# Copies, scalings and block differences go on whichever of two engines the list has free first

## The chip, the cores and the metric

The kernel runs on one core of a Trainium2 chip. A core has a matrix engine (TensorE, PE in the profile; its loading of weights is PEld), three engines for elementwise work (VectorE or DVE, ScalarE or ACT, GpSimd or POOL), a synchronising engine whose queue issues most DMAs (SyncE, SP), an on-chip memory (SBUF) and eight accumulator banks (PSUM). PE writes to the banks; DVE and ACT read them. In this kernel POOL works on SBUF alone. Each engine runs its own instructions in program order and waits on semaphores for the others.

The metric is device time in microseconds of one execution, the median of several runs.

## What is computed

The input x is 16 sequences of 256 tokens with 128 features, in float32. Six residual steps follow, each on a layer norm (no affine) of the running x:

```python
x = x + 0.5 * ffn(norm(x))          # L0: silu(x w1) * (x w2) -> gelu(h h1) -> gelu(h h2) -> w3; 128 -> 512 -> 512 -> 512 -> 128
x = x + nonlocal_attn(norm(x))      # (theta phi^T / sqrt(128)) g, no softmax
x = x + 0.5 * ffn(norm(x))          # the same weights again
x = x + 0.5 * experts(norm(x))      # two of 8 rank-64 experts, chosen by the first token of each sequence
x = x + attention(norm(x))          # 16 heads of 8, rotary positions, causal softmax
x = x + 0.5 * experts(norm(x))
```

Each weight of the feed-forward part is ternary with a scale per output; the attention has scores, a causal mask, softmax, a product with the values and an output projection.

## The kernel before

x stays in SBUF as 32 tiles of 128 tokens. The 16 sequences are worked in nine batches, seven of two sequences (n = 4 tiles, N = 512 tokens wide) and two of one (n = 2, N = 256).

**Feed-forward** (`ffn`, line 329). Features lie on the partitions, tokens along the row. Four chunks give silu(w1) x w2 into `h`. The two 512 x 512 layers are done by a Strassen scheme with seven block products instead of eight (lines 423 on). For it the list needs four differences of blocks of `h`, called T1 to T4 (`sums`, line 360): T1 on DVE, T2 to T4 on POOL; a copy of the first product out of PSUM (`left`, line 384, on ACT); five sums with PSUM (`sum_of`, on DVE, rows `h<-h,pb`); and four gelus on ACT. Each product is four matmuls in the program, eight records in the trace.

**Norms** (`normed`, line 265). DVE makes statistics (`st`, `mv`), POOL makes `nm`, `ve`, `rstd` and `shift` in four small instructions, ACT makes `xn`, one instruction per tile. PE transposes xn and DVE copies the result out of PSUM as `xnT` (`by_feature`, line 280).

**Attention** (`attention`, line 652). PE makes rotated inputs for keys and queries; DVE multiplies by cosine and sine and shuffles pairs, POOL adds (`rotary`, line 633, tile `rot`). From the keys ACT makes four masked planes (`keys`, line 678, rows `qkv<-rot,kone,kmask`), from the queries DVE makes two (`queries`, line 688, rows `qkv<-rot,qmask`). ACT copies the values out of PSUM (`vm`). For each block of scores PE fills four banks; DVE adds the causal mask in PSUM (`pb<-pb,causal`) and takes the row maxima (`mx<-pb`); PE makes the scores again with the maxima folded in, ACT takes the exp (`pr<-pb`), POOL masks (`pr<-pr`) and PE multiplies by the values.

**Non-local attention and experts.** `product` (line 504) makes three small matrices (`gram`, `gph`, `eff`), each copied out of PSUM by DVE. `gated` (line 532) chooses two experts: small DVE instructions, a tanh on ACT, gathers of the expert weights by POOL's own DMA queue (`ab`), and a weight `gw` on DVE.

**The list.** The order of the instructions on each engine is computed while the program is built. Each part above is a generator that yields steps: an engine, a price in us, the banks and buffers it takes and gives back, and what it needs and sets. `begin` (line 927) works out when each waiting step could start on the clock of its engine, and the loop at the end takes the earliest; among PE steps within 0.05 us the feed-forward chain comes last, so it fills what attention leaves. `issue` (line 975) emits the step and moves the engine's clock by the price; what depends on it is ready a `HOP` later (0.24, 0.15, 0.12 and 0.08 us for PE, ACT, DVE and POOL). A step of DVE on N columns is priced at 0.07 + 0.00105 N, of ACT at 0.16 + 0.00083 N, of POOL at 0.19 + 0.0021 N; `sums` prices its POOL steps at 0.05 + 0.002 N. A change of ACT's function table costs 1.28, and an exp that needs one is held back by 2.0 (`PATIENCE`). Nothing in the list tells of one elementwise engine slowing another. `find` (line 914) chooses the bank that is clear first; the first four, which the score blocks need all together, count as `LOAN` = 2.0 us later for anything else while feed-forward work is left. The feed-forward chain (`main`) doesn't use them at all then.

All instructions go out through one wrapper (line 220), which keeps them in the list's order, so nearly every row of the profile has the line L220; rows are told apart by their tiles.

Of the kernel before, what the change touches and what calls it, by code (L numbers as in the profile page):

```python
# [14 lines left out]
AF = mybir.ActivationFunctionType  # L15
# [4 lines left out]
P = 128  # L20
# [4 lines left out]
WARM = 10  # L25
GATHER = 1.15
LANDING = 2.2
LOAN = 2.0
PATIENCE = 2.0
SLACK = 0.05  # L30
HOP = {"PE": 0.24, "ACT": 0.15, "DVE": 0.12, "POOL": 0.08}
# [23 lines left out]
def macaron_kernel(ctx: ExitStack, tc: tile.TileContext, a: dict, out: bass.AP):  # L55
# [169 lines left out]

    def step(engine, us, table=None, banks=0, take=(), drop=(), after=None, needs=(), sets=(), tiles=None, lag=0.0):
        return dict(
            engine=engine, us=us, table=table, banks=banks, take=take, drop=drop, after=after, needs=needs, sets=sets, lag=lag,  # L230
            tiles=tiles,
        )

    def pe(us, **kw):
        return step("PE", us, **kw)
# [29 lines left out]
    def normed(t0, n, needs=()):  # L265
        yield step("DVE", 0.12 + 0.26 * n, needs=needs)
        st = sml.tile([P, GT, 6], F32, name="st")
        for t in range(n):
            nc.vector.bn_stats(st[:, t, :], x[:, t0 + t, :])
        mv = scales(st, n)  # L270
        yield step("POOL", 1.2 + 0.17 * n)
        rstd, shift = inverse(mv, n)
        (xn,) = yield step("ACT", 0.39 * n, take=("xn",))
        for t in range(n):
            nc.scalar.activation(
                xn.t[:, t, :], x[:, t0 + t, :], AF.Identity, bias=shift[:, t : t + 1], scale=rstd[:, t : t + 1]
            )
        return xn

    def by_feature(n, xn, keep=False):  # L280
        pt, xnT = yield pe(0.11 * n, banks=1, take=("xnT",), drop=() if keep else (xn,))
        v = pt.t.rearrange("p (t n) -> p t n", n=P)
        for t in range(n):
            nc.tensor.transpose(v[:, t, :], xn.t[:, t, :], ident)
        yield dve(n * P, drop=(pt,))
        nc.vector.tensor_copy(xnT.t[:, : n * P], pt.t[:, : n * P])
        return xnT

    def first_input(n):
# [39 lines left out]
    def ffn(which, t0, n):  # L329
# [29 lines left out]

        def sums(l, h, T):  # L360

            for i, e, x, y, needs in (
                (1, "DVE", (0, 1), (0, 0), ()),
                (2, "POOL", (1, 1), 1, ()),
                (3, "POOL", (1, 1), (0, 1), ()),
                (4, "POOL", (1, 0), 2, (("P6", l, me),)),
            ):
                needs += tuple(k for b in (x, y) if type(b) is tuple for k in has(l, *b))
                made = (("T", i, l, me),)
                drop = (T[2],) if i == 4 else ()  # L370
                (T[i],) = yield (
                    dve(N, needs=needs, take=("T",), sets=made, drop=drop) if e == "DVE"
                    else step("POOL", 0.05 + 0.002 * N, needs=needs, take=("T",), sets=made, drop=drop)
                )
                engine = nc.vector if e == "DVE" else nc.gpsimd
                engine.tensor_tensor(
                    T[i].t[:, :, :M], block(h, *x), T[y].t[:, :, :M] if type(y) is int else block(h, *y), ALU.subtract
                )

# [3 lines left out]

        def left(l, a, nh):

            yield act(N, sets=(("P1", l, me),))
            nc.scalar.copy(block(nh, 1, 1), in_two(a))

        def shared(l, b, d, nh):

# [108 lines left out]
    def nonlocal_attn(t0, n):  # L499
# [4 lines left out]
        def product(us, lhs, rhs, name, drop=()):  # L504

            (bk,) = yield pe(us, banks=1, drop=drop)
            pp = bk.t[:, : 2 * D].rearrange("p (b d) -> p b d", b=2)
            for b in range(nb):
                if lhs is None:
                    for t in range(2):  # L510
                        v = xn.t[:, 2 * b + t, :]
                        nc.tensor.matmul(pp[:, b, :], v, v, start=(t == 0), stop=(t == 1))
                else:
                    nc.tensor.matmul(pp[:, b, :], lhs[:, b, :], rhs, start=True, stop=True)
            yield dve(nb * D, drop=(bk,))
            m = sml.tile([P, 2, D], F32, name=name, bufs=1)
            nc.vector.tensor_copy(m[:, :nb], pp[:, :nb])
            return m

        gram = yield from product(0.45 * nb, None, None, "gram", (xn,))  # L520
# [72 lines left out]
    def experts(sg):  # L593
        xn = yield from normed(sg.t0, sg.n, (("ffn", 0, (1, sg.t0)), ("ffn", 1, (1, sg.t0)), ("constants",)))
        xnT = yield from by_feature(sg.n, xn)
        if sg.first:
            nb = len(sg.parts)
            yield step("POOL", 0.2 + 0.1 * nb)
            cls = sml.tile([P, 2, P], F32, name="cls", bufs=2)
            nc.gpsimd.tensor_copy(  # L600
                cls[:, :nb],
                xnT.t[:, : sg.n * P].rearrange("p (b s) -> p b s", b=nb)[:, :, 0:1].to_broadcast([P, nb, P]),
            )
            merged["before", sg.g] = yield from gated(nb, cls)
            yield step(None, 0.0, sets=(("before", sg.g),))
        yield from applied(("before", sg.g), sg, xnT)

    def gated_ahead(g, nb, y):
# [14 lines left out]
        pc = bk.t[:, : 2 * D].rearrange("p (b d) -> p b d", b=2)  # L623
        for b in range(nb):
            nc.tensor.matmul(pc[:, b, :], y[:, b, :], ones, start=True, stop=True)
        yield dve(nb * D, drop=(bk,))
        cls = sml.tile([P, 2, P], F32, name="cls", bufs=2)
        nc.vector.tensor_copy(cls[:, :nb], pc[:, :nb])
        merged["after", g] = yield from gated(nb, cls)
        yield step(None, 0.0, sets=(("after", g),))  # L630

# [1 line left out]
    def rotary(c0, N, xnT, n, rot):  # L633
# [10 lines left out]

        yield dve(N)
        nc.vector.stream_shuffle(rot[:, 1, :N], rot[:, 1, :N], [i ^ 1 for i in range(32)])
        yield pool(N)
        nc.gpsimd.tensor_tensor(rot[:, 0, :N], rot[:, 0, :N], rot[:, 1, :N], ALU.add)

    kept = {}  # L650

    def attention(sg):
# [25 lines left out]
        def keys():  # L678


            yield from rotary(c0, N, xnT, 1, rot.t[:, 0:2, :])
            for j in (0, 2, 1, 3):
                yield step("ACT", 0.28 + 0.00083 * N, sets=(("km", sg.t0, j),) + ((("kept", g),) if j == 3 and sg.first else ()))
                nc.scalar.activation(
                    km[:, PLANE[j], c0 : c0 + N], kT[:, :N], AF.Identity, bias=kone[:, j : j + 1], scale=kmask[:, j : j + 1]
                )

        def queries():

            yield from rotary(c0, N, xnT, 0, rot.t[:, 2:4, :])  # L690
            yield step(None, 0.0, sets=(("q", sg.t0),))
            for v in range(2):
                yield step("DVE", 0.15 + 0.0005 * N, sets=(("qz", sg.t0, v),))
                nc.vector.tensor_scalar(qz[:, v, c0 : c0 + N], qT[:, :N], qmask[:, v : v + 1], None, ALU.mult)
            yield step(None, 0.0, needs=(("km", sg.t0, 3),), drop=(rot,))

        spawn(keys())
# [3 lines left out]
        for t in range(n):  # L701
            nc.tensor.matmul(pv[:, t, :], xnT.t[:, t * P : (t + 1) * P], wvT, start=True, stop=True)
        v0 = sg.parts[0][1][0]
        yield step("ACT", 0.53 + 0.225 * n, drop=(bk,), sets=(("v", sg.t0),))
        for i in range(2):
            nc.scalar.copy(
                vm.t[:, v0 : v0 + n].rearrange("p t r (i h) c -> p (t r) i h c", i=2)[:, :, i, :, 16 * i : 16 * i + DK],
                pv[:, :n].rearrange("p t (r i h c) -> p (t r) i h c", i=2, h=2, c=DK)[:, :, i],
            )
# [204 lines left out]
    def find(n, short):  # L914
# [9 lines left out]
        best = min(some, key=lambda b: b.clear + (LOAN if not ended[0] and b in bank[:4] else 0.0))  # L924
        return best.clear, [best], None

    def begin(line):

        n = line.next
# [8 lines left out]
            t = max(t, find(n["banks"], line is not main)[0])  # L938
        if n["table"] == "exp" and table[0] != "exp" and not ended[0]:
            t += PATIENCE  # L940
        return max(t, clock[n["engine"]]) if n["engine"] else t


# [31 lines left out]
    def issue(line):  # L975
# [3 lines left out]
        since, banks, quad = find(n["banks"], line is not main)  # L979
        bufs = [min(store_of[r], key=lambda s: s.clear) for r in n["take"]]  # L980
        t = max([t, since] + [s.clear for s in bufs])
        e, us = n["engine"], n["us"]
        if e:
            if n["table"] and n["table"] != table[0]:
                table[0] = n["table"]
# [156 lines left out]
```

## Time and profile before

| | us |
|---|---|
| median of 3 runs (972.97 to 973.29) | 973.13 |
| the profiled execution: its time | 972.04 |
| its span, first instruction to last | 970.4 |
| PE busy | 918.1 |
| DVE busy | 646.1 |
| ACT busy, of it 77 table loads | 450.2, 98.8 |
| POOL busy | 371.8 |

A row of a group has: line, engine, operation, out<-in by tile name, size of one, x how many, then busy time and mean ns of one, then the engine's idle time ahead of them and what ended it. `pb` is any PSUM bank. The mean is the time from an instruction's start to its end; neighbours on DVE and ACT overlap by some 0.08 to 0.1 us, so their spacing is shorter. A line of waits has who waited, for whom, the total, how many times, and the longest. A line of a stretch has its limits, its length, then busy time of PE, PEld, DVE, ACT and POOL, the granted clock of PE, and the DMA share. A line of the timeline has start, length, engine and instruction. PE's granted clock was full but for the first slices (mean 0.996).

### The profile page before, as it was taken

How to read it: one execution, taken by the hardware profiler on the slowest of the kernel's cores; microseconds unless marked ns; L12 is line 12 of the kernel's file. 1: busy time of each engine (PE TensorE's matmuls, PEld its weight loads, DVE VectorE, ACT ScalarE, POOL GpSimd, SP SyncE). 2: the span in 40 equal slices, each digit the busy share in tenths (PEclk: the TensorE clock that was granted, in tenths of full speed). 3: DMA queues.
4: the chain of work that ended last, by engine and by line, in shares of the span. 5: the costliest groups of instructions: out<-in, count | busy, mean ns of one | idle time of the engine just before them, and what ended most of it. 6: DMA issues, size and time to landing. Idle time of an engine off the chain costs nothing.

```text
span 970.4 us, 16624 instructions
## 1 busy us (share of the span) xinstructions
PE 918.1 (95%) x6600; PEld 690.0 (71%) x6600; DVE 646.1 (67%) x1470; ACT 450.2 (46%) x672; POOL 371.8 (38%) x572
## 2 busy tenths in 40 slices
PE   6999999999999999999999999999999899898887
PEld 4877878666676767686786667767777777786565
DVE  5654456937687646857569376856577676869673
ACT  2244344365535463553552755254652547472342
POOL 5422334241534225341553425242444135343342
PEclk9999999999999999999999999999999999999999
DMA  7000000000000000000000000000000000000000
GB/s 249 16 1 1 1 12 7 5 1 2 12 23 1 1 1 22 12 1 1 13 22 1 2 12 1 23 1 1 12 12 11 1 12 2 23 7 12 1 22 7
DMA packets 14717, 13.76 MB, mean 14 GB/s; under 512 B 2032, under 2 KB 12080, under 8 KB 14640
## 3 DMA queue, kind: packets, MB, share of 16 engines
q1 hardware_dynamic: 12624, 8.11, 2.8%
q0 software_dynamic: 1600, 4.20, 1.5%
q8 instruction: 52, 0.85, 0.4%
q10 hardware_dynamic: 416, 0.39, 0.1%
q14 instruction: 25, 0.20, 0.1%
HBM read 10.60 MB, written 2.10 MB: 13 GB/s over the span
## 4 chain that ended last, share of the span: by engine, by line
PE 65%; DVE 18%; ACT 7%; issue 4%; POOL 3%; DMA 1%; SPq 1%; DVEq 0%; ACTq 0%; POOLq 0%
PE pb L220 65%; DVE mx L220 4%; DVE h L220 3%; ACT pr L220 3%; DVE pb L220 2%; ACT L220 2%; ACT xn L220 1%; POOL rstd L220 1%; DVE st L220 1%; DVE x L220 1%; DMA w3s<-in_w3T_dram 1%; DVE T L220 1%; ACT sil L220 1%; DVE den L220 1%; DVE gw L220 1%
## 5 line engine op out<-in xcount | busy, mean ns | idle before, releaser
L220 DVE TENSOR_TENSOR h<-h,pb 128x512 f32<-128x512 f32 (+1 forms) x180 | 111.9, 622 | 104.4 <-PE pb L220 98.7
L220 PE MATMUL pb<-T,hS 128*128 128x256 f32 (+1 forms) x576 | 134.5, 366 | 10.7 <-DVE h L220 5.8
L220 ACT ACTIVATE h<-h 128x512 f32<-128x512 f32 (+1 forms) x108 | 62.4, 581 | 173.7 <-DVE h L220 173.6
L220 POOL TENSOR_TENSOR T<-h,T 128x512 f32<-128x512 f32 (+1 forms) x72 | 83.7, 1163 | 122.5 <-DVE T L220 56.8
L220 PE MATMUL pb<-qkv 32*128 32x256 f32 (+2 forms) x1536 | 115.1, 405 | 14.9 <-ACT pr L220 7.6
L220 POOL TENSOR_SCALAR nm<-mv 128x4 f32<-128x4 f32 (+3 forms) x62 | 15.1, 243 | 274.1 <-DVE mv L220 267.4
L220 PEld LDWEIGHTS pb<-T,hS 128*128 128x128 f32 x576 | 95.0, 190 | 33.4 <-issue 8.1
L220 ACT ACTIVATE pr<-pb 128x1536 f32<-128x1536 f32 x64 | 92.4, 1449 | 54.6 <-PE pb L220 47.2
L220 ACT ACT_TABLE_LOAD x77 | 98.8, 1283 | 39.2 <-PE pb L220 36.3
L220 POOL TENSOR_SCALAR_AFFINE_SELECT pr<-pr 128x512 f32<-128x512 f32 x128 | 78.2, 635 | 100.0 <-ACT pr L220 99.7
L220 ACT ACTIVATE xn<-x,shift,rstd 128x128 f32<-128x128 f32 x188 | 77.7, 483 | 79.3 <-POOL shift L220 73.6
L220 DVE TENSOR_REDUCE mx<-pb 128x8 f32<-128x2048 f32 (+1 forms) x64 | 111.8, 1750 | 0.5
L220 DVE TENSOR_TENSOR pb<-pb,causal 128x1024 f32<-128x1024 f32 x64 | 78.5, 1227 | 36.1 <-PE pb L220 33.6
L220 PEld LDWEIGHTS pb<-qkv 32*128 32x128 f32 x1536 | 68.2, 184 | 48.1 <-ACT pr L220 16.0
L220 PE MATMUL pb<-xnT,w1T 128*128 128x512 f32 (+1 forms) x144 | 69.0, 561 | 3.0 <-ACT sil L220 1.5
L220 PE MATMUL pb<-xnT,w2T 128*128 128x512 f32 (+1 forms) x144 | 68.7, 559 | 1.3 <-ACT sil L220 1.0
L220 DVE SCALAR_TENSOR_TENSOR h<-pb,s,sil 128x512 f32<-128x512 f32 (+1 forms) x72 | 48.2, 684 | 31.1 <-ACT sil L220 21.2
L220 PE MATMUL pb<-T,h2T 128*128 128x256 f32 (+1 forms) x288 | 64.8, 362 | 3.3 <-DVE T L220 3.0
L220 PE MATMUL pb<-T,h1T 128*128 128x256 f32 (+1 forms) x288 | 66.3, 360 | 0.6 <-DVE T L220 0.6
L220 DVE TENSOR_TENSOR x<-x,pb 128x256 f32<-128x256 f32 (+2 forms) x79 | 37.4, 474 | 43.0 <-PE pb L220 42.8
L220 PE MATMUL pb<-h,h1T 128*128 128x256 f32 (+1 forms) x288 | 65.3, 364 | 0.2 <-DVE h L220 0.2
L220 PE MATMUL pb<-h,hS 128*128 128x256 f32 (+1 forms) x288 | 65.4, 360 | 0.0
(121 smaller groups left out, 1558.3 us busy)
## 6 DMA issues: line engine op xcount, KB each, us to landing
out_dram<-x SPq DMA_DIRECT2D x7, 256.0 KB, 2.3
x<-in_x_dram SPq DMA_DIRECT2D x6, 256.0 KB, 4.7
h1T<-in_h1T_dram SPq DMA_DIRECT2D x1, 1024.0 KB, 9.3
h2T<-in_h2T_dram SPq DMA_DIRECT2D x1, 1024.0 KB, 10.1
ab<-in_eab_dram,at POOLq DMA_INDIRECT x32, 2.8
x<-in_x_dram SPq DMA_DIRECT2D x3, 128.0 KB, 4.9
w1T<-in_w1T_dram SPq DMA_DIRECT2D x1, 256.0 KB, 3.9
w2T<-in_w2T_dram ACTq DMA_DIRECT2D x1, 256.0 KB, 4.1
```

Source lines behind the costliest of these rows:

```text
L220: return lambda *args, **kw: tc.keep_in_program_order(getattr(self.engine, name)(*args, **kw))
```

## The change

A step may now have two forms, each with an engine and a price (`either`). `pick` chooses the form that would end first: the later of the step's readiness and the engine's clock, plus price, plus that engine's hop. It is asked when the list looks for the next step and again when the step is issued. `SPARED`, which would count DVE as later, is 0.

Two forms are given to: xn (ACT 0.39 per tile or DVE 0.21); xnT, gram, gph, eff and one cls, the copies out of PSUM (DVE or ACT); the first product's copy `left` (ACT or DVE); all four differences T (DVE or POOL, POOL now priced 0.19 + 0.0021 N); the other cls (POOL or DVE); the rotary sum (POOL or DVE); the key planes (ACT or DVE); the query scalings (DVE or ACT); and the value copies (ACT 0.53 + 0.225 n or DVE 0.2 + 0.135 n). `LOAN` goes from 2.0 to 1.0. What is computed stays the same.

```diff
-LOAN = 2.0
+LOAN = 1.0
+SPARED = 0.0
...
+    chosen = [None]
+    def either(*alt, **kw):
+        return step(alt[0][0], alt[0][1], alt=alt, **kw)
+    def by():
+        return {"ACT": nc.scalar, "DVE": nc.vector, "POOL": nc.gpsimd}[chosen[0]]
+    def copied(n, **kw):
+        return either(("DVE", 0.07 + 0.00105 * n), ("ACT", 0.16 + 0.00083 * n), **kw)
+    def copy(to, src):
+        if chosen[0] == "ACT":
+            nc.scalar.copy(to, src)
+        else:
+            nc.vector.tensor_copy(to, src)
+    def scaled_by(to, src, scale, bias=None):
+        if chosen[0] == "ACT":
+            nc.scalar.activation(to, src, AF.Identity, scale=scale, **({} if bias is None else {"bias": bias}))
+        elif bias is None:
+            nc.vector.tensor_scalar(to, src, scale, None, ALU.mult)
+        else:
+            nc.vector.tensor_scalar(to, src, scale, bias, ALU.mult, ALU.add)
...
-        (xn,) = yield step("ACT", 0.39 * n, take=("xn",))
+        (xn,) = yield either(("ACT", 0.39 * n), ("DVE", 0.21 * n), take=("xn",))
...
-        yield dve(n * P, drop=(pt,))
-        nc.vector.tensor_copy(xnT.t[:, : n * P], pt.t[:, : n * P])
+        yield copied(n * P, drop=(pt,))
+        copy(xnT.t[:, : n * P], pt.t[:, : n * P])
...
-                (T[i],) = yield (
-                    dve(N, needs=needs, take=("T",), sets=made, drop=drop) if e == "DVE"
-                    else step("POOL", 0.05 + 0.002 * N, needs=needs, take=("T",), sets=made, drop=drop)
+                (T[i],) = yield either(
+                    ("DVE", 0.07 + 0.00105 * N), ("POOL", 0.19 + 0.0021 * N), needs=needs, take=("T",), sets=made, drop=drop
                 )
...
-            yield act(N, sets=(("P1", l, me),))
-            nc.scalar.copy(block(nh, 1, 1), in_two(a))
+            yield copied(N, sets=(("P1", l, me),))
+            copy(block(nh, 1, 1), in_two(a))
...
-        yield pool(N)
-        nc.gpsimd.tensor_tensor(rot[:, 0, :N], rot[:, 0, :N], rot[:, 1, :N], ALU.add)
+        yield either(("POOL", 0.19 + 0.0021 * N), ("DVE", 0.07 + 0.00105 * N))
+        by().tensor_tensor(rot[:, 0, :N], rot[:, 0, :N], rot[:, 1, :N], ALU.add)
...
-                yield step("ACT", 0.28 + 0.00083 * N, sets=(("km", sg.t0, j),) + ((("kept", g),) if j == 3 and sg.first else ()))
+                yield either(("ACT", 0.28 + 0.00083 * N), ("DVE", 0.15 + 0.0005 * N), sets=(("km", sg.t0, j),) + ((("kept", g),) if j == 3 and sg.first else ()))
...
-                yield step("DVE", 0.15 + 0.0005 * N, sets=(("qz", sg.t0, v),))
+                yield either(("DVE", 0.15 + 0.0005 * N), ("ACT", 0.28 + 0.00083 * N), sets=(("qz", sg.t0, v),))
...
-        yield step("ACT", 0.53 + 0.225 * n, drop=(bk,), sets=(("v", sg.t0),))
+        yield either(("ACT", 0.53 + 0.225 * n), ("DVE", 0.2 + 0.135 * n), drop=(bk,), sets=(("v", sg.t0),))
...
+    def pick(n, t):
+        if n["alt"]:
+            n["engine"], n["us"] = min(n["alt"], key=lambda a: max(t, clock[a[0]]) + a[1] + HOP[a[0]] + (SPARED if a[0] == "DVE" else 0.0))
```

## The prediction

> **What bounds the kernel now.** I read the page's busy line first, then busy time by stretch, then what TensorE (PE) waited for in each stretch, then single places in the timeline. The busy line and the chain of the page:
>
> ```profile
> PE 918.1 (95%) x6600; PEld 690.0 (71%) x6600; DVE 646.1 (67%) x1470; ACT 450.2 (46%) x672; POOL 371.8 (38%) x572
> ...
> PE 65%; DVE 18%; ACT 7%; issue 4%; POOL 3%; DMA 1%; SPq 1%; DVEq 0%; ACTq 0%; POOLq 0%
> ```
>
> PE is busy 918.1 of 970.4 us, and the change gives it no work and takes none away. So all there is to win is PE's idle time, 52.3 us. What there is to lose is open. Busy time by stretch (columns PE, weight loads, DVE, ACT, POOL) places it:
>
> ```profile
> 0.00:20.00 20.00, 12.08 (x39) 7.91 (x40) 8.75 (x32) 4.95 (x10) 9.98 (x21) 0.93 0.73 241
> 20.00:750.00 730.00, 712.07 (x4672) 528.97 (x4674) 484.03 (x1084) 345.25 (x516) 283.83 (x410) 1.00 0.03 9
> 750.00:850.00 100.00, 92.16 (x810) 74.10 (x806) 73.00 (x172) 53.00 (x84) 35.83 (x63) 0.98 0.03 9
> 850.00:970.40 120.40, 101.80 (x1084) 79.00 (x1084) 80.35 (x184) 46.98 (x64) 42.13 (x80) 1.00 0.04 10
> ```
>
> The idle time is 7.9 us at the start, 17.9 in the long middle, 7.8 in 750 to 850 and 18.6 at the end, where no feed-forward work is left to fill gaps. Waits of PE in the middle, and then behind 750:
>
> ```profile
> PE pb L220 <- DVE h L220: 5.0, 6, 1.5
> PE pb L220 <- DVE mx L220: 2.5, 5, 0.8
> PE pb L220 <- DVE T L220: 2.2, 3, 0.9
> PE pb L220 <- POOL T L220: 2.2, 4, 0.9
> ...
> PE pb L220 <- ACT pr L220: 7.8, 10, 1.6
> PE pb L220 <- DVE mx L220: 5.9, 8, 1.1
> PE pb L220 <- ACT sil L220: 2.4, 3, 0.9
> ```
>
> VectorE (DVE) is the engine PE waits for most, and the one that the change loads. Over the whole span PE's waits for DVE are 8.4 (mx), 6.4 (h), 3.6 (T), 2.0 (x), 0.6 (y), 0.5 (qkv), 0.5 (ab), 0.4 (xnT) and 0.3 (oT): 22.7 us.
>
> **What moves, and how much.** The list now compares two engines by the later of readiness and engine clock, plus price and hop. With both free it takes DVE for nearly everything: xn of four tiles 0.84+0.12 against 1.56+0.15 on ACT; a key plane 0.41+0.12 against 0.70+0.15; a difference T or the rotary sum 0.61+0.12 against 1.27+0.08 on POOL; a 512-wide copy 0.73 against 0.74, a tie that goes to whichever clears first. So xn leaves ACT unless DVE is 0.75 us further behind than ACT. At the 53 ends of `shift` in the timeline (what xn waits for) DVE was free or within 0.75 us of free in 50; I take 85% of xn, 75% of key planes, T, rotary sums and value copies, half of the copies of P1 to DVE, and 40% of the DVE copies out of PSUM to ACT.
>
> ```profile
> L220 ACT ACTIVATE xn<-x,shift,rstd 128x128 f32<-128x128 f32 x188 | 77.7, 483 | 79.3 <-POOL shift L220 73.6 <-DMA rot<-in_woT_dram 5.5
> L220 POOL TENSOR_TENSOR T<-h,T 128x512 f32<-128x512 f32 x56 | 72.0, 1285 | 107.9 <-DVE T L220 49.3 <-PE pb L220 34.5 <-ACT h L220 12.3
> L220 DVE COPY xnT<-pb 128x512 f32<-128x512 f32 x41 | 27.8, 683 | 20.8 <-PE pb L220 20.7
> ```
>
> DVE's price for each comes from its own rows, as spacing of neighbours: the xn of the first input, on DVE already, start 6.1 to 6.8 for four, 0.24 each (ACT: four in 1.65, 0.41 each); a 512-wide two-operand instruction 0.60 (367.93 to 368.53), a 256-wide 0.34; the scaling qkv<-rot 0.48. So DVE gains 160 xn x 0.24 = 38.4; 21 planes x 0.48 + 6 x 0.27 = 11.7; 63 T x 0.61 + 18 x 0.34 = 44.5; rotary 10 x 0.61 + 3 x 0.34 = 7.1; P1 copies 14 x 0.61 + 4 x 0.34 = 9.9; values about 4. It gives away 16 xnT x 0.61 + 5 x 0.34 + 11 small copies x 0.34 = 15.2. Net +100 us: DVE 646 to 746, 67% to 77%. ACT loses about 80, POOL about 107. No DMA is moved and SP's queue is untouched; POOL's gathers (32, 33.9 us) stand behind fewer T.
>
> **Gains, place by place.** At 208.06 and 545.04 PE waits 0.95 each for T, behind an ACT queue that began with four xn (198.43, 1.65 us), a table load and gelu. With xn on DVE, which must finish mx and then still has h to make, gelu comes 0.8 earlier: 1.6. The four waits for POOL's T (0.40, 0.55, 0.87, 0.39) each lose up to 1.28 - 0.61 = 0.67: 2.0. Before 280.57 and 617.55 PE waits 0.54 for mx, which stood behind a gw of 1.04 (0.16 where undisturbed) that ran beside POOL's T: 1.1. At 651.70 the exp stands behind four xn: 0.6. Late, DVE puts two query scalings (0.34 each) and a cls copy (0.28) between causal adds and maxima that PE waits for; ACT idles there: 1.0. The last norm's two xn: 0.3. Together 6.6. What is late next at these places is the rest of each wait and then DVE's queue.
>
> **Costs.** More work on DVE. Of the 22.7 us of waits for DVE 3.7 are counted as gains; on the other 19.0 the load acts. Lower bound 0 (the list orders PE's work with the new load known, and a gap in the middle is filled with matmuls that stand ready). Upper bound by busy over idle, 0.77/0.23 against 0.67/0.33, 1.67 times: +12.7. I take them in proportion to busy time, 746/646: +2.9, nearer the lower end since in the middle 484 us of DVE work cause 9.7 us of waits.
>
> DVE held by POOL. The timeline shows what the list doesn't know:
>
> ```profile
> 364.47 1.34 DVE L220 TENSOR_SCALAR gw<-ew 128x2 f32<-128x2 f32 x1
> 364.50 1.28 POOL L220 TENSOR_TENSOR T<-h,T 128x512 f32<-128x512 f32 x1
> ...
> 365.82 1.59 PEld L220 LDWEIGHTS pb<-T,hS 128*128 128x128 f32 x8 [0.95 <-POOL T L220]
> 365.82 1.99 PE L220 MATMUL pb<-T,hS 128*128 128x256 f32 x8 [0.55 <-POOL T L220]
> ```
>
> A scaling of two columns took 1.34 us, just as long as the POOL subtraction beside it. Over their medians, gw lost (516-182) x 14 = 4.7 us, the query scalings (579-480) x 14 = 1.4, and T of 128x256 (533-418) x 8 = 0.9; T of 128x512 nothing. That is 7.0 us in some 68 instructions, 0.1 each. The moved work makes about 40 groups of xn, 27 planes, 81 T and 13 sums: 161 x 0.1 = 16 us of DVE time that the list doesn't plan. PE bears from none of it to all, 0 to 16; behind a held DVE instruction stand, in order, the sums h and the maxima that PE's next product needs. Of DVE's present 646 us PE feels 22.7, 3.5%, and by that 0.5; I take this, since POOL loses the T and sums, which hold longest.
>
> The Trainium skill has a rule that speaks against the change: "SBUF — State Buffer", section Who interferes with whom, says that VectorE and GpSimd share a port pair as an exclusive lock, taken by a two-port scaling or a read of two SBUF operands, and that the later one fully blocks. The gw row agrees. By that rule every xn that meets POOL is held for the rest of POOL's instruction, and the sum would be that of the second rival below.
>
> At the start, xn of the second batch (15.90) would meet POOL's weight scaling (1.26 us from 15.82): 0 to +0.6, I take 0.3. LOAN at 1.0 lets short work borrow the score banks sooner: at most the waits it could spare (sil 3.4 and h 6.4) or lengthen (pr 9.3, mx 8.4); the profile doesn't say which, so 0. POOL's corrected price for T (1.07 to 1.27, measured 1.27) costs nothing by itself. An xn on ACT needs no table load (the four at 178.35 and those at 180.48 stand among sil with none), so the 77 loads change only with the order.
>
> Sum: -6.6 + 2.9 + 0.5 + 0.3 = **-2.9 us**. The profiled execution took 972.04 (span 970.4 and 1.6 around it), 1.1 below the median of 973.13; so 969.1 on its terms and **970.2** against the median.
>
> **Rivals.** First, more in the tail: 26.4 us of PE's idle time lie behind 750, and if the shorter chains there (planes on two engines, xn at 0.24) halve the 5.9 us for mx and spare 1.5 of pr, another 4.4 goes: 965.8. Against it: before 898.39, 920.61 and 945.32 ACT had nothing but the exp itself, so nothing moved off it helps.
>
> Second, slower: DVE held by POOL. Its place is xn right behind `shift`: at 18 of the 53 ends POOL's next subtraction or mask starts within 0.1 us, so DVE's first scaling meets it, and h, mx and causal queue behind. If 55% of the 16 us reach PE, the sum is -6.6 + 2.9 + 8.8 + 0.3 = +5.4: 978.5. It decides from where PE bears over 3.4 of the 16 us (21%). For it: PE's matmuls stand in a fixed order, and attention's are placed the moment the list thinks them ready, so lateness that it didn't plan shows at once. Against it: T of 128x512 never lost anything.
>
> Third, no difference: the list mostly fills time that PE doesn't wait in, or second engines are rarely taken where PE waits: 973.1.
>
> **How the numbers follow.** Under 0.2%, 1.95 us, this kernel can't be told from no change. Forecast 0.42 (its own range 965 to 971), tail 0.06, no difference 0.13, held and crowded DVE 0.39 (975 to 985, the crowding bound of 12.7 inside). So faster 0.48, same 0.13, slower 0.39. The range goes from 962 (gains with no cost at all, 966.5, and the tail's 4.4) to 981, leaving out some 0.05 below and 0.10 above. Cases of both signs hold most of the chance; the change is near to even.
>
> **What would show it.** DVE busy near 746 and 77%, ACT near 370, POOL near 265; xn rows on DVE some 160. Right: the waits for POOL T gone and for ACT sil and pr in the middle shorter, DVE waits up by no more than 3. Wrong: scalings xn whose mean is far above 0.35 us (held), PE's waits for DVE h and mx above 20 us, or idle time behind 750 grown beyond 26.

## The result and the profile after

The changed kernel takes 960.88 us (960.41 to 962.17 in four runs) against 973.05 for the kernel before, measured beside it: ratio 0.9878, 95% interval 0.9866 to 0.9891. The forecast was 970.2 with a range of 962 to 981. The direction was right; the gain of 12.2 us is four times the 2.9 forecast and lies 1.1 us outside the range. The profiled execution took 962.17, its span is 960.5. The busy line and the chain of the page after:

```profile
PE 919.9 (96%) x6572; PEld 687.5 (72%) x6572; DVE 730.5 (76%) x1688; ACT 409.5 (43%) x550; POOL 278.5 (29%) x480
...
PE 74%; DVE 17%; ACT 3%; issue 3%; POOL 1%; DMA 1%; SPq 0%; POOLq 0%; DVEq 0%; ACTq 0%
```

PE has the same work (919.9 against 918.1), DVE carries 84 us more, ACT 41 and POOL 93 less. PE's idle time is now 960.5 - 919.9 = 40.6 us instead of 52.3. By stretch (limits, length, then PE, PEld, DVE, ACT, POOL, clock):

```profile
0.00:20.00 20.00, 9.37 (x34) 5.99 (x34) 8.98 (x27) 3.23 (x5) 9.63 (x20) 0.90 0.76 237
20.00:750.00 730.00, 722.94 (x4714) 536.56 (x4714) 561.78 (x1274) 319.01 (x426) 199.22 (x333) 1.00 0.03 9
750.00:850.00 100.00, 90.21 (x839) 71.05 (x838) 81.82 (x205) 52.35 (x71) 33.10 (x59) 1.00 0.03 9
850.00:960.50 110.50, 97.39 (x990) 73.92 (x988) 77.91 (x187) 34.91 (x49) 36.57 (x69) 0.96 0.04 11
```

Idle time against before: start 7.9 to 10.6, the middle 17.9 to 7.1, 750 to 850 from 7.8 to 9.8, the end 18.6 to 13.1. The middle gains most, the start loses. What PE waits for in 20 to 750 of the kernel after (who, for whom: total, times, longest):

```profile
PE pb L221 <- DVE mx L221: 2.6, 4, 1.7
PE pb L221 <- DVE oT L221: 1.1, 1, 1.1
PE pb L221 <- DVE xn L221: 1.1, 2, 0.9
PE pb L221 <- ACT pr L221: 1.0, 3, 0.6
```

The waits for POOL's T (2.2 before), DVE's T (2.2), x (2.0) and h (5.0) are gone or down to 0.2. And over the whole span:

```profile
PE pb L221 <- DVE mx L221: 10.5, 12, 2.0
PE pb L221 <- DVE xn L221: 9.7, 5, 7.0
PE pb L221 <- ACT pr L221: 3.5, 7, 0.9
```

The wait of 7.0 for xn is the start. The moved groups, by form (busy time, mean ns | idle time ahead):

```profile
L221 DVE TENSOR_SCALAR xn<-x,rstd,shift 128x128 f32<-128x128 f32 x142 | 48.9, 418 | 8.3 <-POOL shift L221 8.1
L221 DVE TENSOR_TENSOR T<-h,T 128x512 f32<-128x512 f32 x48 | 39.4, 821 | 8.5 <-PE pb L221 5.0 <-POOL T L221 1.8 <-issue 0.9
L221 ACT ACTIVATE xn<-x,shift,rstd 128x128 f32<-128x128 f32 x46 | 19.1, 482 | 28.8 <-POOL shift L221 28.8
L221 DVE TENSOR_SCALAR gw<-ew 128x2 f32<-128x2 f32 x14 | 2.5, 180 | 0.0
```

The weight gw, 516 ns before, takes 180: POOL's T no longer runs beside it. But an undisturbed xn on DVE takes 340 ns (the median), so 142 of them at a mean of 418 lose 142 x 78 = 11 us. This product, (mean - 340) x count, is called **the loss of xn** below. T loses too: of the T on DVE nine of 128x512 took 0.96 to 1.79 instead of 0.69, 6.9 us more in all. The timeline shows one (start, length):

```profile
187.34 1.27 POOL L221 TENSOR_TENSOR T<-h 128x512 f32<-128x512 f32 x1 [3.17 <-DVE h L221]
187.37 1.79 DVE L221 TENSOR_TENSOR T<-h,T 128x512 f32<-128x512 f32 x1
```

One h released both engines; POOL began 0.03 us ahead, and DVE's difference lasted 1.1 us longer than alone (0.69). Last the start, where xn of the second batch now is on DVE:

```profile
16.04 0.20 POOL L221 TENSOR_TENSOR shift<-nm,rstd 128x4 f32<-128x4 f32 x1
16.19 1.26 POOL L221 TENSOR_TENSOR h1T<-h1T,rot 128x512 f32<-128x512 f32 x1
16.27 4.61 DVE L221 TENSOR_SCALAR xn<-x,rstd,shift 128x128 f32<-128x128 f32 x4 [1.18 <-POOL shift L221]
17.39 1.80 POOL L221 MEMSET vm<- 128x2048 f32 x1
19.16 1.29 POOL L221 TENSOR_TENSOR h1T<-h1T,rot 128x512 f32<-128x512 f32 x1
19.33 0.69 PE L221 MATMUL pb<-ident,xn 128*128 128x128 f32 x2 [6.96 <-DVE xn L221]
```

Four scalings take 4.61 us beside three POOL instructions; before, ACT made the four in 1.65. PE's first product of the 512 x 512 layers (`pb<-h,h1T`) starts at 27.15 instead of 22.63.

So the result holds a gain and, inside it, a loss that the forecast had named. The experiments were meant to price both.

### The profile page after: what moved, and what is told of

Read it like the earlier page. It is cut to its first block, busy times and chain, and to the rows that moved or that the text cites. A ratio compares the mean times of both kernels' runs of the same rounds, so it can differ in the third digit from the quotient of the medians.

```text
span 960.5 us, 16511 instructions
## 1 busy us (share of the span) xinstructions
PE 919.9 (96%) x6572; PEld 687.5 (72%) x6572; DVE 730.5 (76%) x1688; ACT 409.5 (43%) x550; POOL 278.5 (29%) x480
## 4 chain that ended last, share of the span: by engine, by line
PE 74%; DVE 17%; ACT 3%; issue 3%; POOL 1%; DMA 1%; SPq 0%; POOLq 0%; DVEq 0%; ACTq 0%
PE pb L221 74%; DVE mx L221 3%; DVE pb L221 3%; DVE h L221 2%; ACT pr L221 1%; DVE xn L221 1%; DVE rot L221 1%; ACT L221 1%; DMA x<-in_x_dram 1%; DVE x L221 1%; DVE T L221 1%; DVE qkv L221 1%; DVE st L221 1%; POOL rstd L221 1%; DVE inv L221 0%
## 5 line engine op out<-in xcount | busy, mean ns | idle before, releaser
L221 POOL TENSOR_SCALAR_AFFINE_SELECT pr<-pr 128x512 f32<-128x512 f32 x128 | 80.2, 651 | 147.1 <-ACT pr L221 145.2
L221 POOL TENSOR_SCALAR nm<-mv 128x4 f32<-128x4 f32 (+3 forms) x62 | 17.7, 286 | 359.4 <-DVE mv L221 358.1
L221 ACT ACTIVATE sil<-pb,s 128x512 f32<-128x512 f32 (+1 forms) x72 | 45.4, 639 | 64.3 <-PE pb L221 63.9
L221 PE MATMUL pb<-h,h2T 128*128 128x256 f32 (+1 forms) x288 | 64.1, 361 | 0.0
L221 PE MATMUL pb<-w3s,h 128*128 128x128 f32 x512 | 63.3, 277 | 0.0
L221 PEld LDWEIGHTS pb<-w3s,h 128*128 128x128 f32 x512 | 60.7, 192 | 3.1 <-issue 1.5
```

What stands on the lines that cost most here:

```text
L221: return lambda *args, **kw: tc.keep_in_program_order(getattr(self.engine, name)(*args, **kw))
```

## The experiments

All times are medians; a ratio is against the kernel before, run beside the kernel. Two more columns divide each profiled span. **F** is the time at which 448 of the 512 records of the feed-forward's last layer (`pb<-w3s,h`) are done, so nearly all the work that fills gaps; **rest** is the span behind F, mostly attention and experts alone. Both come from the one profiled execution, which isn't always a typical one: it lies 4.8 us above the median for b4_copies_fixed, 2.7 above for b2_xn_alone and 2.9 below for b3_price_alone.

| kernel | us | ratio (95%) | xn on DVE | loss of xn, us | F, us | rest, us |
|---|---|---|---|---|---|---|
| before | 973.05 | 1 | 0 | 0 | 761.5 | 208.9 |
| **after** | 960.88 | 0.9878 (0.9866 to 0.9891) | 142 | 11 | 754.6 | 205.9 |
| b1_T_alone | 963.37 | 0.9900 (0.9881 to 0.9919) | 0 | 0 | 752.8 | 209.8 |
| b2_xn_alone | 989.44 | 1.0162 (1.0119 to 1.0205) | 140 | 23 | 783.9 | 206.6 |
| b3_price_alone | 977.89 | 1.0044 (1.0029 to 1.0060) | 0 | 0 | 759.7 | 213.5 |
| a2_loan1_alone | 979.26 | 1.0067 (1.0048 to 1.0086) | 0 | 0 | 762.8 | 214.4 |
| a3_xn_on_act | 969.34 | 0.9970 (0.9956 to 0.9985) | 0 | 0 | 755.6 | 211.8 |
| a4_T_fixed | 986.77 | 1.0135 (1.0118 to 1.0152) | 176 | 23 | 779.0 | 208.2 |
| b4_copies_fixed | 985.08 | 1.0114 (1.0094 to 1.0133) | 162 | 21 | 780.2 | 207.9 |
| a1_loan2 | 983.83 | 1.0112 (1.0095 to 1.0129) | 160 | 19 | 764.1 | 217.2 |
| n1_before_slack | 973.97 | 1.0003 (0.9993 to 1.0013) | 0 | 0 | 761.4 | 211.7 |
| n2_after_slack | 981.73 | 1.0076 (1.0051 to 1.0100) | 158 | 18 | 770.4 | 209.6 |
| d3_T_alone_slack | 965.24 | 0.9929 (0.9912 to 0.9945) | 0 | 0 | 749.4 | 213.1 |
| d4_xn_on_act_slack | 966.99 | 0.9935 (0.9917 to 0.9954) | 0 | 0 | 753.5 | 213.6 |
| c1_list_knows_hold | 961.69 | 0.9894 (0.9876 to 0.9912) | 92 | 2 | 754.8 | 203.8 |
| c2_first_xn_act | 957.78 | 0.9850 (0.9831 to 0.9869) | 138 | 6 | 751.3 | 204.2 |
| d1_hold_slack | 979.44 | 1.0071 (1.0054 to 1.0088) | 96 | 3 | 757.2 | 221.2 |
| d2_hold_loan2 | 974.74 | 1.0017 (1.0007 to 1.0026) | 122 | 5 | 760.9 | 210.9 |
| e1_ten_idle_matmuls | 978.56 | 1.0058 (1.0041 to 1.0075) | 96 | 3 | 757.3 | 219.8 |
| e2_first_xn_act_fill | 958.66 | 0.9860 (0.9844 to 0.9877) | 138 | 6 | 751.3 | 205.1 |

### One part alone, in the kernel before

T alone (`either` and `pick` as in the change):

```diff
-                (T[i],) = yield (
-                    dve(N, needs=needs, take=("T",), sets=made, drop=drop) if e == "DVE"
-                    else step("POOL", 0.05 + 0.002 * N, needs=needs, take=("T",), sets=made, drop=drop)
+                (T[i],) = yield either(
+                    ("DVE", 0.07 + 0.00105 * N), ("POOL", 0.19 + 0.0021 * N), needs=needs, take=("T",), sets=made, drop=drop
                 )
```

> The kernel before with only the four differences T free to go to VectorE or GpSimd, at the new price; LOAN stays at 2.0. Theory Q: the waits for POOL T (2.2) and a good part of those for DVE T and h in the middle (7.2) go, 966 to 970. Rival B: only the 2.2 of POOL T, 970.5 to 972. Rival O: 965 to 980.

Only POOL's price for T:

```diff
-                    else step("POOL", 0.05 + 0.002 * N, needs=needs, take=("T",), sets=made, drop=drop)
+                    else step("POOL", 0.19 + 0.0021 * N, needs=needs, take=("T",), sets=made, drop=drop)
```

> The kernel before, with T2 to T4 still on GpSimd but priced at 0.19 + 0.0021 N as in the change (1.27 us for 512 columns, as measured, instead of 1.07). Theory H (T alone wins because the work leaves GpSimd): 971 to 976. Rival P (T alone won because the list was told the right price): 962 to 966.

T alone gives 963.4, nearly the whole gain; the price alone gives none (977.9). Middle stretch and gw of the kernel with T alone:

```profile
20.00:750.00 730.00, 717.38 (x4712) 535.51 (x4711) 527.04 (x1160) 346.14 (x516) 204.08 (x341) 1.00 0.03 9
...
L220 DVE TENSOR_SCALAR gw<-ew 128x2 f32<-128x2 f32 x14 | 2.2, 158 | 0.0
```

PE idles 12.6 in the middle instead of 17.9. 118 of the 144 differences went to DVE, PE waits for no T of POOL any more, and gw is undisturbed (158 ns).

xn alone:

```diff
-        (xn,) = yield step("ACT", 0.39 * n, take=("xn",))
+        (xn,) = yield either(("ACT", 0.39 * n), ("DVE", 0.21 * n), take=("xn",))
```

> The kernel before with only xn free to go to ScalarE or VectorE; LOAN stays at 2.0. Some 140 of 188 xn are then on VectorE. Theory Q: the start loses 4 to 5 us (xn held on VectorE by GpSimd, as in the changed kernel), and the middle wins 2 to 4: 972 to 976. Rival B: the start loses the same and nothing is won: 977 to 979.

It costs 16 us (four runs, 985.2 to 993.2). Group by form, then PE's waits in 20 to 750, then the first of PE's waits over the whole span, of this kernel:

```profile
L220 DVE TENSOR_SCALAR xn<-x,rstd,shift 128x128 f32<-128x128 f32 x140 | 58.2, 504 | 12.2 <-POOL shift L220 12.1
...
PE pb L220 <- DVE xn L220: 9.5, 12, 2.9
PE pb L220 <- issue: 5.9, 4, 1.5
PE pb L220 <- DVE x L220: 4.8, 5, 1.0
...
PE pb L220 <- DVE xn L220: 18.0, 15, 6.7
```

An xn lasts 504 ns instead of 340, and PE, which never waited for xn in the middle of the kernel before, waits 9.5 us for it there. F comes 22 us later. Not all of the loss is waiting: of the 20 us by which this profiled execution is longer than the one before, 11.3 are more idle time of PE and 8.8 more busy time (926.9 against 918.1), at a mean granted clock of 0.980 against 0.996. This is the rival "DVE held by POOL", far larger than it was priced.

LOAN alone:

```diff
-LOAN = 2.0
+LOAN = 1.0
```

> The kernel before with LOAN at 1.0 and nothing else. Theory Q (queues: the gain comes from work taken out of the queues of ScalarE and GpSimd ahead of what TensorE waits for): no gain, 971 to 975. Rival B (banks: short work that borrows the score banks sooner leaves the four banks of the feed-forward chain free, and the 7.0 us of middle waits for DVE h and DVE x are waits for a bank): 966 to 969, with those two waits at most 2 us together. Rival O (any new order moves the time by several us): anywhere from 965 to 980.

979.3. The middle stays nearly as it was (waits for h 5.0, F 762.8); 5.5 us are in the rest. I had put 0.

### One part undone, in the changed kernel

```diff
-        (xn,) = yield either(("ACT", 0.39 * n), ("DVE", 0.21 * n), take=("xn",))
+        (xn,) = yield either(("ACT", 0.39 * n), take=("xn",))
```

> The changed kernel with every xn on ScalarE, as before the change; all other choices stay. Theory H (VectorE held by GpSimd: xn on VectorE loses more than it wins, T on VectorE wins because it takes away what holds and what TensorE waits for): the start wins its 4.5 us and the middle loses little, 953 to 958. Rival Q (the middle won because ScalarE's queue lost the xn): start wins, middle loses 5 or more, 961 to 966.

```diff
-                    ("DVE", 0.07 + 0.00105 * N), ("POOL", 0.19 + 0.0021 * N), needs=needs, take=("T",), sets=made, drop=drop
+                    ("DVE", 0.07 + 0.00105 * N) if i == 1 else ("POOL", 0.19 + 0.0021 * N),
+                    needs=needs, take=("T",), sets=made, drop=drop
```

> The changed kernel with T1 on VectorE and T2 to T4 on GpSimd again, at the corrected price of 0.19 + 0.0021 N; all other choices stay. Theory H: xn meets GpSimd's subtractions again, the xn rows lose 20 us or more over their median, and the time is 980 to 992, slower than the kernel before. Rival Q: only the gain of T alone is given back, 968 to 972.

```diff
-        return either(("DVE", 0.07 + 0.00105 * n), ("ACT", 0.16 + 0.00083 * n), **kw)
+        return either(("DVE", 0.07 + 0.00105 * n), **kw)
...
-            yield copied(N, sets=(("P1", l, me),))
+            yield either(("ACT", 0.16 + 0.00083 * N), sets=(("P1", l, me),))
```

> The changed kernel with the copies out of PSUM fixed as before (xnT, gram, gph, eff, cls on VectorE, the first product on ScalarE); xn, T, planes, rotary sum and values stay free. If the copies are worth nothing in the sum: 957 to 965. If the 25 or so copies that went to ScalarE are what keeps VectorE from crowding: 966 to 972.

```diff
-LOAN = 1.0
+LOAN = 2.0
```

> The changed kernel with LOAN back at 2.0. LOAN alone cost the kernel before 7 us, nearly all of it behind 850 us. If that is what LOAN does, the changed kernel gains as much: 953 to 956. If it was only the luck of one order (rival O), the time is anywhere within 8 us of 961, on either side.

Each undoing makes the changed kernel slower, and three make it slower than before: 986.8 (T), 985.1 (copies), 983.8 (LOAN). Read naively, every part would be worth 8 to 26 us, far more together than the whole change gives. With T back on POOL the result is that of xn alone (gw again at 692 ns, F 779.0). But the copies and LOAN move no work to or from POOL, and still xn lost 21 and 19 us there. That raised the question of whether the changed kernel's own order was a lucky one.

### The same kernels in another order

The list treats PE steps within 0.05 us as simultaneous (`SLACK`). Making that 0.06 means nothing for the work and gives another order.

```diff
-SLACK = 0.05
+SLACK = 0.06
```

The kernel before:

> The kernel before with SLACK at 0.06 instead of 0.05, a change of the list that has no meaning for any engine. It shows what a new order alone does. If order alone moves little: 970 to 976. If it moves as much as the parts of the change did (rival O): 7 us or more away from 973.

The kernel after:

> The changed kernel with SLACK at 0.06 instead of 0.05. If order alone moves little: 957 to 965. Rival O: 7 us or more away from 961; the 23 us between LOAN 1.0 and 2.0 in the changed kernel would then be such an accident, and no proof on LOAN.

T alone:

> The kernel before with only T free, with SLACK at 0.06 (with 0.05 it took 963.4). If the gain of T is a property of the move: 960 to 968. If it was an accident of one order: 969 to 980.

The changed kernel with xn on ACT:

> The changed kernel with every xn on ScalarE and SLACK at 0.06. With xn free it took 981.7 at this SLACK; with xn on ScalarE and SLACK 0.05 969.3. If the hold of xn is the cause of the 20 us: 963 to 972. If the order is: 976 to 985.

The kernel before stays (974.0), T alone stays a gain (965.2), and so does the change without its xn (967.0). The change as a whole goes from 960.9 to 981.7, from a gain to a loss. Its xn row in the new order:

```profile
L221 DVE TENSOR_SCALAR xn<-x,rstd,shift 128x128 f32<-128x128 f32 x158 | 58.5, 455 | 14.4 <-POOL shift L221 14.3
```

The loss of xn is 18 instead of 11 us, F is 16 us later, and in the middle PE again waits for mx (6.0), h (5.7) and xn (3.4). So what the change does to the time is not one number: T is a gain in both orders; xn, with T free, is worth 8.5 us in one (960.9 against 969.3) and costs 14.7 in the other (981.7 against 967.0).

### Is it the hold?

Two edits attack the hold itself. The first moves one group: the second batch's xn, the four that took 4.61 us at the start, back to ACT.

```diff
-    def normed(t0, n, needs=()):
+    def normed(t0, n, needs=(), alts=("ACT", "DVE")):
...
-        (xn,) = yield either(("ACT", 0.39 * n), ("DVE", 0.21 * n), take=("xn",))
+        (xn,) = yield either(*(a for a in (("ACT", 0.39 * n), ("DVE", 0.21 * n)) if a[0] in alts), take=("xn",))
...
-        xn = yield from normed(t0, n, needs)
+        xn = yield from normed(t0, n, needs, ("ACT",) if (which, t0) == (0, 2 * FIRST[1]) else ("ACT", "DVE"))
```

> The changed kernel, but the xn of the second batch (the one for which TensorE waits 7.0 us at the start) stays on ScalarE, as in the kernel before. If GpSimd's hold on VectorE costs the start its 4.5 us (first product of the first layer at 27.15 against 22.63 us), the time is 956 to 957.5, with that product at 22.4 to 23. If the lost start is made up later anyway (TensorE has ready work to catch up with), it stays at 960 to 961.5.

957.8, just above what was expected: the first 512 x 512 product starts at 23.9 instead of 27.15, and F comes 3.3 earlier (751.3). A repeat of the same program (below) took 958.7. This is the fastest of all, 1.4 to 1.5% under the kernel before.

The second teaches the list. A DVE step between SBUF tiles that may move (marked 1: xn, T, the rotary sum, planes, query scalings, cls) now waits for POOL's clock, and POOL's next step for its end:

```diff
-        (xn,) = yield either(("ACT", 0.39 * n), ("DVE", 0.21 * n), take=("xn",))
+        (xn,) = yield either(("ACT", 0.39 * n), ("DVE", 0.21 * n, 1), take=("xn",))
...
+    held = [0.0]
+    def free(e, both):
+        if e == "POOL":
+            return max(clock[e], held[0])
+        return max(clock[e], clock["POOL"]) if both else clock[e]
...
-            n["engine"], n["us"] = min(n["alt"], key=lambda a: max(t, clock[a[0]]) + a[1] + HOP[a[0]] + (SPARED if a[0] == "DVE" else 0.0))
+            a = min(n["alt"], key=lambda a: max(t, free(a[0], len(a) > 2)) + a[1] + HOP[a[0]])
```

> The changed kernel with a list that knows of the hold: a movable step that reads SBUF alone on VectorE (xn, T, planes, query scalings, rotary sum, one cls) starts no earlier than GpSimd's clock, and GpSimd starts nothing before such a step ends. Theory H: the choice then sends xn to ScalarE where GpSimd is at work; what xn loses over its median falls from 10.7 us to under 4, the start wins its 4.5, and the time is 952 to 957. Rival O: another order, 957 to 968.

With SLACK at 0.06 as well:

> The list that knows of the hold (the changed kernel, LOAN 1.0), with SLACK at 0.06. The changed kernel without that knowledge took 981.7 at this SLACK. If the hold is what costs the 20 us: xn loses under 4 us to it and the time is 956 to 967. If the order is the cause and the hold only goes along with it: 973 to 985.

With LOAN at 2.0 as well:

> The list that knows of the hold, with LOAN at 2.0. Without that knowledge the time was 983.8. If the hold is the cause: 956 to 967. If LOAN or the order is: 973 to 985.

The xn row of c1_list_knows_hold, and then of d1_hold_slack:

```profile
L221 DVE TENSOR_SCALAR xn<-x,rstd,shift 128x128 f32<-128x128 f32 x92 | 27.5, 360 | 7.0 <-POOL shift L221 6.8
```

```profile
L221 DVE TENSOR_SCALAR xn<-x,rstd,shift 128x128 f32<-128x128 f32 x96 | 30.0, 374 | 8.1 <-POOL shift L221 7.9
```

The list now sends a third to a half of the xn to ACT and the rest to DVE at moments when POOL is quiet; the loss of xn falls to 2 to 5 us. In the two orders where the hold was dear, F falls with it: 770.4 to 757.2 at SLACK 0.06, 764.1 to 760.9 at LOAN 2.0. In the change's own order it doesn't: the loss falls from 11 to 2 and the first 512 x 512 product starts at 22.77 instead of 27.15, but F stays (754.6 and 754.8), and so does the time (961.7 against 960.9). Over all kernels with T free, F is 749 to 756 where xn lost nothing, 751 to 761 where it lost 2 to 11, and 764 to 780 where it lost 18 to 21. So a dear hold goes with a late F, but not in proportion. As each of these edits also gives another order, how much of the middle's loss is the hold's own isn't shown.

The times at the other SLACK and LOAN are a miss: 979.4 and 974.7, the first only 2.3 below the same SLACK without this knowledge. In d1_hold_slack the middle's 13 us came back and the rest gave 11.6 of them away: 221.2 us, the longest of all.

### The end

In that end the clock looked like the cause. Stretches of d1_hold_slack (the granted clock stands behind the five busy times), and one row of its timeline:

```profile
866.80:870.20 3.40, 0.42 (x12) 0.11 (x1) 3.40 (x3) 0.00 (x0) 0.00 (x0) 0.91 0.01 2
870.20:883.80 13.60, 10.77 (x55) 8.03 (x56) 12.55 (x35) 3.11 (x7) 3.02 (x6) 0.50 0.04 11
883.80:887.20 3.40, 3.40 (x34) 2.64 (x37) 0.82 (x3) 1.25 (x2) 1.44 (x2) 0.58 0.00 0
...
870.48 0.81 PE L221 MATMUL pb<-qkv 32*128 32x256 f32 x4 [3.26 <-DVE mx L221]
```

The clock falls to half within one wait of 3.26 us and stays there for some 17 us: by the rows' means 0.6 us of the first, all 13.6 of the second and 2.9 of the third. Ten matmuls of the identity, which nothing reads, were put into that wait:

```diff
                 awake(t)
+                if near[0] and n["banks"] == 4:
+                    fours[0] += 1
+                    if fours[0] == 7:
+                        for _ in range(10):
+                            nc.tensor.matmul(min(bank[4:], key=lambda s: s.clear).t[:, :P], ident, ident, start=True, stop=True)
```

> d1 (the list knows of the hold, SLACK 0.06, 979.4 us) with ten matmuls of the identity put on TensorE ahead of the one score block for which it waits 3.26 us near 867 us; they take some 2.2 us and nothing reads them. If the half clock after that wait is what costs: the granted clock of 870 to 890 us is 0.9 or more instead of 0.58 and the time falls by 6 to 9 us, to 970 to 973. If the order there is what costs: 978 to 981.

The same stretch without the matmuls (first fence, d1_hold_slack) and with them (second, e1_ten_idle_matmuls, with two rows from inside it):

```profile
870.00:890.00 20.00, 16.54 (x120) 12.29 (x124) 14.59 (x41) 6.04 (x9) 5.68 (x10) 0.58 0.03 7
```

```profile
870.00:890.00 20.00, 13.97 (x124) 9.97 (x128) 14.75 (x41) 6.24 (x9) 5.68 (x10) 0.74 0.02 7
873.60:877.00 3.40, 1.34 (x8) 0.90 (x6) 3.40 (x8) 0.66 (x2) 0.00 (x0) 0.96 0.00 0
877.00:883.80 6.80, 3.88 (x24) 2.88 (x25) 5.83 (x21) 2.55 (x5) 1.82 (x2) 0.50 0.07 22
```

The clock rose from 0.58 to 0.74, not to the 0.9 that was expected, and PE was busy 2.6 us less there; the kernel took 978.6 instead of 979.4. The matmuls put the fall off, from within the wait to just before 877, and the half clock then lasted some 10 us instead of 17. What PE saved until then it waited: 1.86 for `rot` at 875.59 and 1.71 for `lg` at 878.51, both on DVE, which is busy for 14.6 to 14.8 of the 20 us in either kernel. So the first 7 us of half clock did not hold up this end; what the other 10 cost was not tested.

The last edit lets the kernel's own filler, which puts identity matmuls into long waits once the last work is on its way, begin earlier in c2_first_xn_act:

```diff
-        if idle > 0.0 and ended[0] and free.clear < clock["PE"]:
+        if idle > 0.0 and (ended[0] or near[0]) and free.clear < clock["PE"]:
```

> c2 (the changed kernel with the second batch's xn on ScalarE, 957.8 us) where the list may also fill TensorE's idle time, as it does after the last feed-forward matmul, from the moment the last feed-forward slot is the next. If the clock costs c2 some 2 us (0.91 in 930 to 950): 954 to 957. If the filling only stands in the way: 958 to 963.

The list saw no such wait, and no matmul was added: PE's order is that of c2_first_xn_act, and the run tells nothing of filling. It is a second measurement of that kernel, 958.7.

What makes the end 204 us long in one order and 221 in another is not settled. Price alone, LOAN alone and T alone in its second order also lengthened it by 4 to 6 us against the kernel before, without any xn on DVE. The clock has a part in some of them. The stretch behind F, of the kernel before and of LOAN alone:

```profile
761.50:970.40 208.90, 182.46 (x1822) 143.80 (x1820) 143.07 (x343) 97.58 (x144) 77.96 (x143) 0.99 0.04 10
```

```profile
762.80:977.30 214.50, 188.60 (x1837) 147.68 (x1835) 143.56 (x343) 97.96 (x144) 78.06 (x143) 0.96 0.04 10
```

LOAN alone doesn't make PE wait longer there (25.9 us idle against 26.4); PE is busy 6.1 us longer, at a clock of 0.96 instead of 0.99. In d1_hold_slack the clock behind F is 0.92, PE is busy 6.8 longer and idle 5.5 longer than before. But the end of the price alone is long (213.5) at the same 0.99 as before, so the clock isn't the whole of it. (In the kernel before, too, the clock was not full everywhere behind its start: 0.98 in 750 to 850.)

## Why the prediction was right or wrong

**Loads: right for DVE and POOL, half right for ACT.** DVE was forecast at 746 and is 730.5, POOL at 265 and is 278.5; ACT at 370 and is 409.5, so it lost 41 us instead of 80. 142 xn went to DVE (160 said), 106 of 144 T, 10 of the 14 wide rotary sums; only 12 of the planes (27 said).

**Gains: the term for T was too small. This is the step that put the forecast too high.** I wrote "The four waits for POOL's T each lose up to 0.67: 2.0" and gw 1.1, together 3.1. T alone gave 9.7 us in one order and 6.9 in the other (ratios 0.9900 and 0.9929 of 973). The trace showed the waits put down to POOL's T; under that name it didn't show that the same POOL instructions also held DVE's scalings (gw 516 to 158 ns) and what stands behind them on DVE. How T's gain divides between the shorter T and the freed DVE was not measured apart and stays open.

**Gains: the terms for xn have no fixed sign.** I counted 1.6 at the two waits behind ACT, 0.6 for the exp and 0.3 at the last norm. xn alone is +16 us. In the changed kernel's own order it comes out ahead by 8.5 us, but by the profiled executions 1.0 of this lies ahead of F and 5.9 in the end, and it is no property of xn, since at SLACK 0.06 the same exchange costs 14.7. At LOAN 2.0 and with fixed copies xn loses as much (19 and 21 us) and F is late too (764.1 and 780.2), though the same kernels with xn on ACT were not run.

**Luck.** T alone gives 9.7 us, the whole change without xn 2.9 (0.9970), with xn 12.2. In the other order it is 6.9, 6.3 (0.9935) and a loss of 7.4. So T's gain held in both orders tried, the other parts together added nothing to it, and what xn brought on top came from an order that happened to suit it. That part is luck, and so is it that the forecast had the direction right: at SLACK 0.06 the same change loses.

**Cost, DVE held by POOL: mechanism right, size wrong.** The sign that was named for it came: xn's mean is 418 ns. I took 0.5 of a range of 0 to 16, by the share of DVE's busy time that PE feels, and because "POOL loses the T and sums, which hold longest". The 16 us were about right as DVE time (11 for xn and 7 for T in the changed kernel, 18 to 23 for xn where it went badly). What failed here is the 3.5%, and it erred to the other side, hiding part of T's gain: PE's transpose waits for xn directly, and `xnT` and a layer follow it. With xn alone xn lost 23 us, and PE's waits for xn over the span came to 18.0 instead of 4.8, 13.2 more: over half, and not 3.5%. (The gw row that was read as agreeing shows that gw was held, and not which came first: gw's record starts at 364.47, POOL's at 364.50.) The argument "T of 128x512 never lost anything" failed as well: before, T1 on DVE and T2 to T4 on POOL followed one another; now one h can release two T at once, and the later one is held (1.79 us).

**Start: wrong.** 0 to +0.6, 0.3 taken, for meeting one POOL instruction. It met three, and the first layer starts 4.5 us later. Putting that one xn on ACT gave back 3.1 (957.8).

**More work on DVE: wrong for the middle.** I added 2.9 in proportion to busy time. Over the span the waits for DVE went from 22.7 to 25.9, +3.2, but 9.7 of those are xn, 7.0 at the start; in the middle all the others fell from about 12 to 4. How busy DVE is did not set what PE waits; which instruction is held or late did. Why h fell from 5.0 to 0.2 in this order, but stayed at 4.8 with T alone and at 5.7 at SLACK 0.06, is open.

**LOAN and price at 0.** Alone they cost some 6 and 4 us. In the profiled executions 5.5 and 4.6 us of it lie in the end (rest 214.4 and 213.5 against 208.9); that of the price is one of its quick runs (974.95) and has F 1.8 earlier. As reordering by itself moves the end by as much (T alone: rest 209.8 and 213.1), neither can be told from a change of order.

**The rivals.** The slower one, 978.5 from the hold, did not come about here, but three near variants of the change end there or somewhat above: 981.7 (SLACK), 983.8 (LOAN kept at 2.0) and 985.1 (copies fixed). "More in the tail" is only partly right: the idle time behind 750 fell from 26.4 to 22.9, but the waits for mx there rose from 5.9 to 7.9. The forecast's near-even chances described the change better than its single number; its range was too narrow below, as it summed named waits and gave no room for what the order itself does.

## What to carry to other kernels

Before moving work to the engine with the shorter instruction, look at what runs beside it: where a row's mean is well above its median, the timeline shows which engine's instruction ends together with the long ones. Moving work away from the holder (T) can be worth more than the waits put down to it, while moving a chain's first step under it (xn) can cost more than the whole average suggests. In a kernel whose order is computed from prices, repeat each variant under a meaningless reordering before believing in a gain of 1%: here the change itself went from -1.2% to +0.8%, T alone stayed a gain, and undoing single parts gave differences that may be no more than orders. A list that chooses among engines should know which of them exclude each other; giving it that knowledge cut the loss of xn from 18 to 3 us, though the time followed by only 2.3, as the end grew.

## What the runs showed that was not expected

**A memset holds a scaling on DVE too.** At 17.39 POOL only wrote `vm`, for 1.80 us, with no tile read, and two of DVE's scalings ended only behind it, at 19.27 and 19.34. It doesn't hold every DVE instruction: in the kernel before, DVE's product `h1T<-h1T,rot` took its 0.68 us beside the same memset. And the hold outlasts one POOL instruction: the first xn took 3.00 us, through the multiplication and the memset, and PE could transpose two of the four at 19.33, when the memset was over, and the other two only at 20.87, after POOL's next multiplication. The Trainium skill, "SBUF — State Buffer", section Who interferes with whom, describes VectorE's second port pair as shared with GpSimd under an exclusive lock; these lengths agree with it. What the runs add is a price: with xn held like this, moving xn alone was a loss of 16 us.

**A half clock of 17 us began within one wait of 3.26 us, and 7 us less of it gained 0.9 us.** In d1_hold_slack the row 866.80 to 870.20 has a mean of 0.91, which is half clock for its last 0.6 us; so the clock fell at about 869.6, some 2.4 us into the wait. With ten matmuls in that wait it fell only near 876.7, in a stretch where PE was busy for 1.34 of 3.40 us. The Trainium skill, "TensorE: Matmul & The Clock Gate", section What's actually happening, has a free-running window of about 3.4 us and half rate after an idle one. Both falls came with PE busy for a part of the last 3.4 us, so here a window did not have to be wholly idle; how idle it has to be, no run here shows. What the slower clock is worth depends on who PE waits for next: the 7 us that were spared went into waits for DVE.
